# A fused attention and convolution block: the depthwise convolution and the line scans spread over VectorE, ScalarE and GpSimd

## The chip, the cores and the metric

The kernel runs on one core of one Trainium2 chip. The metric is the device time of one execution in microseconds, lower is better; three executions were timed. The engines are called PE (TensorE), DVE (VectorE), ACT (ScalarE), POOL (GpSimd) and SP (SyncE, which here issues all DMAs).

## The reference

Two layers work on `x` of shape (2, 56, 56, 384), all in float32. Layer 0 is neighborhood attention (12 heads, 7 x 7 window) and an MLP with GELU; it is not touched by the change except for one detail of its norm. Layer 1 is what matters:

```
def _L1_conv_ref(x, n1_g, n1_b, w_in, b_in, k_conv, on_g, on_b, w_out, b_out, n2_g, n2_b, w1, b1, w2, b2):
    h = _layernorm(x, n1_g, n1_b)
    p = h @ w_in + b_in                      # 384 -> 768 channels
    local = conv_general_dilated(p, k_conv, padding='SAME', feature_group_count=768)   # 3 x 3, depthwise
    lr = _ema_scan(local, axis=2)            # y[t] = 0.6 y[t-1] + 0.4 x[t], along the row
    rl = _ema_scan(local, axis=2, reverse=True)
    tb = _ema_scan(local, axis=1)            # down the column
    bt = _ema_scan(local, axis=1, reverse=True)
    mixed = 0.25 * (lr + rl + tb + bt) + local
    mixed = _layernorm(mixed, on_g, on_b)
    x = x + (mixed @ w_out + b_out)
    h2 = _layernorm(x, n2_g, n2_b)
    return x + gelu(h2 @ w1 + b1) @ w2 + b2
```

## The kernel before

The program has an attention part (about the first 1010 us of the span) and then two passes over the 6272 tokens in 13 groups of 512 (the last has 128).

*First half (layer 0's MLP and layer 1's projection in).* For each group: `hidden` makes 12 tiles of 128 hidden channels (PE, line L569, evicted with GELU by ACT at L578), `tokens` multiplies them back (L585, four tiles of 128 tokens, DVE adds the residual into `xc` at L720), the result is normed (`Norm`, `finish`) and, one group later, `project_in` makes six tiles of 128 channels of `p` (L569 again, evicted by ACT at L691) and stores them to `p_d` in DRAM. `Norm.add` takes statistics on DVE (L144, L145), `close` computes the reciprocal root (L149 on DVE, `pow` on POOL at L150), `apply` norms on DVE (L154).

*Second half.* `load_mix` brings the mixed image back, `measure` transposes it (L753) and takes statistics, `project_out` multiplies by `w_out` (L585, L765), then come norm, `hidden`, `tokens` and the output (L804). `add_row` adds a bias row on POOL (L518).

*The convolution* of one image is `phase_c(b)`: a Python generator that runs over six tiles of 128 channels. Each tile holds the whole 56 x 56 image per channel. Per tile: the image is loaded (`pt`); the centre tap is a product on DVE (L629, two halves of 28 rows); eight more taps are multiply-adds on DVE into `loc` (L640, each in two halves); ACT copies `loc` turned, in four pieces, into the buffer of `pt`, now called `lt` (L651); DVE scans 14 lines at a time forwards (L606), scales the line ends (L609), scans backwards in place (L611) and adds the share of it to `loc` (`mix`, L617: along rows from `both`, along columns with a stride from `lt`); the result goes to `mix_d` (L666). `loc` and `pt` share three buffers under the tag `image`.

*The order.* `Beside` mixes the generator's steps into the program behind the matmul work: `beside.go(worth)` credits 0.9 of the matmul time, and each `yield` debits the time of a step. `begin(phase_c(0))` stands in `project_in` where image 0 of `p` is complete (L701), `begin(phase_c(1))` at L783, behind `project_out(0)`; `end()` (L775, L799) flushes what is left before its result is loaded. The scheduling pass behind the language then orders each engine's queue by its own estimate, so the trace shows the norm's statistics between taps. Engines run their queues in order.

Of the kernel before, what the change touches and what calls it, by code (L numbers as in the profile page):

```python
# [104 lines left out]
def block_kernel(ctx: ExitStack, tc: tile.TileContext, ins: dict, out: bass.AP):  # L105
# [18 lines left out]
    nc.sync.dma_start(out=chan, in_=ins["chan"])  # L124
    mhalf = const.tile([P, NT], F32, name="mhalf")
    nc.vector.memset(mhalf, -0.5)

    def col(name, i=0):
        return chan[:, COL[name] + i : COL[name] + i + 1]

    class Norm:
# [14 lines left out]

        def close(self, k, n=P):
            rs = self.rs[:n, :k]
            nc.vector.tensor_scalar_add(rs, self.mv[:n, :k, 1], EPS)  # L149
            nc.gpsimd.tensor_tensor(rs, rs, mhalf[:n, :k], ALU.pow)  # L150

        def apply(self, k, x, out):
            n = x.shape[0]
            nc.vector.tensor_scalar(  # L154
                out, x, self.mv[:n, k, 0:1], self.rs[:n, k : k + 1], ALU.subtract, ALU.mult
            )

    def to_channels(psum, xs, dst, nch, g, b):
# [346 lines left out]
    nc.sync.dma_start(out=w_in, in_=ins["L1_conv_w_in"].rearrange("(c p) n -> p c n", p=P))  # L505
    load_w2(w2, s2)
    xs[1] = load_group(x1f, 1, "xa")
    rows = wp.tile([P, 3, C], F32, name="rows")
    for r in range(3):
        nc.sync.dma_start(out=rows[:, r, :], in_=ins["rows"][r + 2 : r + 3, :].to_broadcast([P, C]))  # L510
    w_out = wp.tile([P, NI, C], F32, name="w_out")
    nc.sync.dma_start(out=w_out, in_=ins["L1_conv_w_out"].rearrange("(c p) n -> p c n", p=P))

    def row(name):
        return rows[:, ROWS[name] - 2, :]

    def add_row(x, n, name):
        nc.gpsimd.tensor_tensor(  # L518
# [15 lines left out]
    def prepare_w_out():  # L534


        wide = wp.tile([P, P], F32, name="wide")
        ps = ps_y.tile([P, C], F32, name="y")
        for c in range(NI):
            nc.vector.tensor_copy(wide, col("L1_conv_on_b", c).to_broadcast([P, P]))  # L540
            nc.tensor.matmul(ps, lhsT=wide, rhs=w_out[:, c, :], start=c == 0, stop=c == NI - 1)
        nc.vector.tensor_tensor(row("b_out"), ps, row("b_out"), ALU.add)
        ps = ps_y.tile([P, C], F32, name="y")
        mean = wp.tile([P, P], F32, name="mean")
        nc.vector.memset(mean, 1.0 / INNER)
        for c in range(NI):
            nc.vector.tensor_scalar_mul(w_out[:, c, :], w_out[:, c, :], col("L1_conv_on_g", c))
            nc.tensor.matmul(ps, lhsT=mean, rhs=w_out[:, c, :], start=c == 0, stop=c == NI - 1)
        for c in range(NI):
            nc.vector.tensor_tensor(w_out[:, c, :], w_out[:, c, :], ps, ALU.subtract)  # L550

    def finish(norm, x, n):

        norm.close(n)
        xn = io.tile([P, NT, C], F32, name="xn")
        for k in range(n):
            norm.apply(k, x[:, k, :], xn[:, k, :])
        return xn

    def channels(xn, n, g, b):  # L560
# [13 lines left out]

    def hidden(w1, m, hT, n, b1):
        ps = columns(w1, m, hT, n)
        t = gp.tile([P, MT], F32, name="hid")
        nc.scalar.activation(t[:, : n * P], ps[:, : n * P], AF.Gelu, bias=col(b1, m))  # L578
        return t

# [9 lines left out]

    def phase_c(b):

        def load(m):
            t = cp.tile([P, H, W], F32, name="pt", tag="image")
            nc.sync.dma_start(out=t.rearrange("p h w -> p (h w)"), in_=p_d[b][m])
            return t

        tail = 1.0 / (1.0 - DECAY * DECAY)
        share = 0.25 * GAIN / tail / (1.0 + 0.5 * GAIN)

        def both_ways(dst, line):
            flat = dst.rearrange("p a b -> p (a b)")
            nc.vector.tensor_tensor_scan(  # L606
                flat, decay, line.rearrange("p a b -> p (a b)"), 0.0, ALU.mult, ALU.add
            )
            nc.vector.tensor_scalar_mul(dst[:, :, W - 1 :], dst[:, :, W - 1 :], tail)  # L609
            yield 2.1  # L610
            nc.vector.tensor_tensor_scan(  # L611
                flat[:, ::-1], decay, flat[:, ::-1], 0.0, ALU.mult, ALU.add
            )
            yield 1.8

        def mix(dst, s):
            nc.vector.scalar_tensor_tensor(dst, s, share, dst, ALU.mult, ALU.add)  # L617

        ready = load(0)
        for m in range(NI):  # L620
            pt = ready
            loc = cp.tile([P, H, W], F32, name="loc", tag="image")

            def tap(dy, dx):
                i = ((dy + 1) * 3 + dx + 1) * NI + m
                return taps[:, i : i + 1]

            for r in range(0, H, H // 2):
                nc.vector.tensor_scalar_mul(  # L629
                    loc[:, r : r + H // 2], pt[:, r : r + H // 2], tap(0, 0)  # L630
                )
                yield 1.0
                for dy in (-1, 0, 1):
                    for dx in (-1, 0, 1):
                        if dy == 0 and dx == 0:
                            continue
                        lo, hi = max(r, -dy), min(r + H // 2, H - max(0, dy))
                        xs, xt = max(0, -dx), max(0, dx)
                        n = W - abs(dx)
                        nc.vector.scalar_tensor_tensor(  # L640
                            loc[:, lo:hi, xs : xs + n], pt[:, lo + dy : hi + dy, xt : xt + n],
                            tap(dy, dx), loc[:, lo:hi, xs : xs + n], ALU.mult, ALU.add,
                        )
                        yield 1.8
            if m + 1 < NI:
                ready = load(m + 1)

            lt = pt.rearrange("p h w -> p (h w)").rearrange("p (w h) -> p w h", h=H)
            cuts = [slice(i, i + LINES) for i in range(0, W, LINES)]
            for i in cuts:  # L650
                nc.scalar.copy(lt[:, i, :], loc[:, :, i].rearrange("p h w -> p w h"))  # L651
            done = None
            for i in cuts:
                both = cp.tile([P, LINES, W], F32, name="both", bufs=2)
                yield from both_ways(both, loc[:, i, :])
                if done is not None:
                    mix(*done)
                    yield 1.0
                done = loc[:, i, :], both
            mix(*done)  # L660
            yield 1.0
            for i in cuts:
                yield from both_ways(lt[:, i, :], lt[:, i, :])
                mix(loc[:, :, i].rearrange("p h w -> p w h"), lt[:, i, :])
                yield 1.6
            nc.sync.dma_start(out=mix_d[b][m], in_=loc.rearrange("p h w -> p (h w)"))  # L666


# [16 lines left out]
    def project_in(g, xn):  # L685
        t0, n = groups[g]
        hT = channels(xn, n, "L1_conv_n1_g", "L1_conv_n1_b")
        pt = io.tile([P, NI, MT], F32, name="mx")
        for m in range(NI):
            ps = columns(w_in, m, hT, n)  # L690
            nc.scalar.activation(  # L691
                pt[:, m, : n * P], ps[:, : n * P], AF.Identity, bias=col("L1_conv_b_in", m)
            )
            beside.go(PRO)
        for b, at, here, n in images(t0, n * P):
            nc.sync.dma_start(
                out=p_d[b][:, :, at : at + n].rearrange("m p t -> p m t"),
                in_=pt[:, :, here : here + n],
            )
            if at + n == T1 and b == 0:  # L700
                beside.begin(phase_c(0))  # L701
# [73 lines left out]
    beside.end()  # L775
    ahead = load_mix(0)
    project_in(*waiting)
    load_w2(w2, s2)
    for k in range(groups[0][1]):
        measure(ahead[0], ahead[2], k)  # L780
    ahead[2].close(groups[0][1])
    x3, xn = project_out(0, *ahead)
    beside.begin(phase_c(1))  # L783
    ahead = load_mix(1)
    for k in range(groups[1][1]):
        measure(ahead[0], ahead[2], k)
# [2 lines left out]
    for g, (t0, n) in enumerate(groups):  # L789
        hid = []  # L790
        for m in range(NHID):
            hid.append(hidden(w1, m, hT, n, "L1_conv_b1"))
            beside.go(MLP)
        res = x3
        if g < last:
            x3, xn = project_out(g + 1, *ahead)
        if g + 2 <= last:
            if groups[g + 2][0] + groups[g + 2][1] * P > T1:
                beside.end()  # L799
            ahead = load_mix(g + 2)  # L800
        for k in range(n):
            ps = tokens(hid, w2, k)
            o = io.tile([P, C], F32, name="o")
            nc.vector.tensor_tensor(o, ps, res[:, k, :], ALU.add)  # L804
            nc.sync.dma_start(out=yout[t0 + k * P : t0 + (k + 1) * P, :], in_=o)
            if g + 2 <= last and k < groups[g + 2][1]:
                measure(ahead[0], ahead[2], k)
            beside.go(ROW)
        if g + 2 <= last:
            ahead[2].close(groups[g + 2][1])  # L810
        if g < last:
            hT = channels(xn, groups[g + 1][1], "L1_conv_n2_g", "L1_conv_n2_b")
# [62 lines left out]
```

## Time and profile before

| | |
|---|---|
| median of 3 runs | 3246.63 us (3242.19 to 3247.16) |
| profiled execution, its own time | 3243.59 us |
| its span, first to last instruction | 3241.5 us |
| PE busy | 2961.1 us, 91% |
| DVE busy | 1673.4 us, 52% |
| ACT busy | 934.0 us, 29% |
| POOL busy | 405.2 us, 13% |
| convolution taps on DVE, L640 | 338.3 us, 192 instructions |
| waits of ACT's turned copies (L651) for the taps | 219.3 us, 9 times |

Busy time is the union of an engine's instructions; a busy engine may be waiting inside an instruction. "Idle before" names what the engine waited for. In a row such as `loc<-pt,taps,loc` the output tile stands first. `128x784` is 128 partitions by 784 elements, that is 14 lines of 56. Durations of one DVE instruction overlap the next by some 0.08 us in the records.

### The profile page before, as it was taken

How to read it: one execution, taken by the hardware profiler on the slowest of the kernel's cores; microseconds unless marked ns; L12 is line 12 of the kernel's file. 1: busy time of each engine (PE TensorE's matmuls, PEld its weight loads, DVE VectorE, ACT ScalarE, POOL GpSimd, SP SyncE). 2: the span in 40 equal slices, each digit the busy share in tenths (PEclk: the TensorE clock that was granted, in tenths of full speed). 3: DMA queues.
4: the chain of work that ended last, by engine and by line, in shares of the span. 5: the costliest groups of instructions: out<-in, count | busy, mean ns of one | idle time of the engine just before them, and what ended most of it. 6: DMA issues, size and time to landing. Idle time of an engine off the chain costs nothing. (4 is left out here: it accounts for less than half of the span.)

```text
span 3241.5 us, 35452 instructions
## 1 busy us (share of the span) xinstructions
PE 2961.1 (91%) x13647; PEld 1621.3 (50%) x13647; DVE 1673.4 (52%) x3371; ACT 934.0 (29%) x2269; POOL 405.2 (13%) x277
## 2 busy tenths in 40 slices
PE   6999999999987999999998668688787799999999
PEld 3555555555554555555554334444444455555555
DVE  3555555555562111111199999689999951111110
ACT  1555555455562222222222122221022111111111
POOL 2310123300031000000001000011110111111000
PEclk9999999999998999999999889798988899999999
DMA  6222222211123111111212211332221121111000
GB/s 136 74 59 64 64 64 77 62 54 58 60 63 120 39 39 39 39 39 39 79 40 79 98 59 52 108 134 79 76 74 47 42 76 39 39 39 39 17 10 13
DMA packets 105673, 197.03 MB, mean 61 GB/s; under 512 B 7408, under 2 KB 81120, under 8 KB 102432
## 3 DMA queue, kind: packets, MB, share of 16 engines
q1 hardware_dynamic: 105504, 194.77, 18.4%
q8 instruction: 107, 1.75, 0.2%
q14 instruction: 62, 0.51, 0.0%
HBM read 117.68 MB, written 77.07 MB: 60 GB/s over the span
## 5 line engine op out<-in xcount | busy, mean ns | idle before, releaser
L585 PE MATMUL y<-w,hid 128*128 128x384 f32 x2352 | 786.9, 494 | 58.2 <-DVE xc L720 58.2
L569 PE MATMUL mm<-hT,w 128*128 128x512 f32 (+1 forms) x1872 | 770.4, 572 | 7.5 <-ACT hid L578 4.6
L585 PEld LDWEIGHTS y<-w,hid 128*128 128x128 f32 x2352 | 450.1, 194 | 365.4 <-DVE xc L720 61.8
L569 PEld LDWEIGHTS mm<-hT,w 128*128 128x128 f32 x1872 | 346.1, 192 | 418.4 <-issue 395.9
L578 ACT ACTIVATE hid<-mm,chan 128x512 f32<-128x512 f32 (+1 forms) x312 | 206.1, 663 | 850.2 <-PE mm L569 850.2
L346 ACT ACTIVATE pr<-pr,nm 112x238 f32<-112x238 f32 (+3 forms) x672 | 326.8, 488 | 227.2 <-DVE nm L339 224.2
L150 POOL TENSOR_TENSOR rs<-rs,mhalf 128x4 f32<-128x4 f32 (+2 forms) x66 | 85.9, 1302 | 2023.6 <-DVE rs L149 1978.6
L640 DVE SCALAR_TENSOR_TENSOR loc<-pt,taps,loc 128x1485 f32<-128x1485 f32 (+2 forms) x192 | 338.3, 1803 | 0.0
L339 DVE CUSTOM_DVE_ANT_0 pr<-sc,bias 112x238 f32<-112x238 f32 (+3 forms) x672 | 240.6, 407 | 171.6 <-PE sc L330 167.2
L167 ACT ACTIVATE hT<-tp,chan 128x512 f32<-128x512 f32 (+2 forms) x159 | 110.0, 744 | 669.5 <-PE tp L164 645.5
L720 DVE TENSOR_TENSOR xc<-y,xa 128x384 f32<-128x384 f32 x49 | 27.0, 551 | 500.5 <-PE y L585 500.5
L585 PE MATMUL y<-w_out,mx 128*128 128x384 f32 x588 | 208.4, 510 | 40.1 <-DVE xc L765 40.1
L360 PE MATMUL pt<-ident,pr 112*100 112x112 f32 (+5 forms) x1584 | 210.4, 272 | 10.2 <-ACT pts L365 10.2
L232 PE MATMUL tp<-hT,wqkv 128*128 128x448 f32 x504 | 211.9, 553 | 8.1 <-DVE qT L238 5.4
L569 PE MATMUL mm<-hT,w_in 128*128 128x512 f32 (+1 forms) x468 | 194.3, 574 | 18.1 <-ACT mx L691 18.1
L360 PEld LDWEIGHTS pt<-ident,pr 112*100 112x100 f32 (+5 forms) x1584 | 163.7, 148 | 82.1 <-issue 53.4
L765 DVE SCALAR_TENSOR_TENSOR xc<-y,rs,xa 128x384 f32<-128x384 f32 x49 | 29.8, 609 | 303.9 <-PE y L585 302.8
L585 PEld LDWEIGHTS y<-w_out,mx 128*128 128x128 f32 x588 | 115.7, 200 | 124.6 <-DVE xc L765 44.4
L164 PE MATMUL tp<-ident,xn 128*128 128x128 f32 (+1 forms) x609 | 88.1, 290 | 83.9 <-DVE xn L154 51.5
L330 PE MATMUL sc<-kT,qT 32*112 32x238 f32 (+3 forms) x1344 | 158.1, 418 | 0.0
L569 PEld LDWEIGHTS mm<-hT,w_in 128*128 128x128 f32 x468 | 87.2, 192 | 120.7 <-issue 93.1
L404 PE MATMUL tp<-wproj,oT 128*112 128x384 f32 x336 | 129.8, 525 | 15.7 <-DVE qT L238 14.7
(70 smaller groups left out, 2710.1 us busy)
## 6 DMA issues: line engine op xcount, KB each, us to landing
pt<-p_d SPq DMA_DIRECT2D x12, 1568.0 KB
mix_d<-loc SPq DMA_DIRECT2D x12, 1568.0 KB
xa<-x_d SPq DMA_DIRECT2D x24, 768.0 KB
p_d<-mx SPq DMA_DIRECT2D x11, 1536.0 KB
mx<-mix_d SPq DMA_DIRECT2D x11, 1536.0 KB
xg<-in_x SPq DMA_DIRECT2D x14, 672.0 KB
v_d<-vs SPq DMA_DIRECT2D x56, 168.0 KB
xr<-in_x SPq DMA_DIRECT2D x56, 168.0 KB
```

Of the source, the lines that this page charges most:

```text
L164: nc.tensor.transpose(tp[:, k * n : (k + 1) * n], x[:, c * P : (c + 1) * P], ident[:n, :n])
L167: nc.scalar.activation(dst[:, c, : len(xs) * n], tp, AF.Identity, bias=col(b, c), scale=col(g, c))
L232: nc.tensor.matmul(ps, lhsT=wqkv[:, c, m * P : (m + 1) * P], rhs=hT[:, c, :], start=c == 0, stop=c == NC - 1,)
L330: nc.tensor.matmul(ps[:, : w.nk], lhsT=qTs[w.b, w.g][d, hg, w.j, :], rhs=kT[d, hg, w.r0 : w.r0 + w.kr, w.c0 : w.c0 + w.kc], start=True, st ...
L339: nc.vector.tensor_tensor_reduce(out=self.pr[:, i, : w.nk], in0=ps[:, : w.nk], in1=w.bias[:, 4 * hg + i, : w.nk], scale=-1.0, scalar=BIG, ...
L346: nc.scalar.activation(self.pr[:, i, : w.nk], self.pr[:, i, : w.nk], AF.Exp, bias=nm[:, i : i + 1], scale=-1.0, accum_out=w.sums[:, h : h ...
L360: nc.tensor.transpose(tp[:n, i, :], self.pr[:, i, a : a + n], idt)
L404: nc.tensor.matmul(ps, lhsT=w.oT[:, c, :], rhs=wproj[:, c, :], start=c == 0, stop=c == NC - 1)
L569: nc.tensor.matmul(ps[:, : n * P], lhsT=w[:, c, m * P : (m + 1) * P], rhs=hT[:, c, : n * P], start=c == 0, stop=c == NC - 1,)
L578: nc.scalar.activation(t[:, : n * P], ps[:, : n * P], AF.Gelu, bias=col(b1, m))
L585: nc.tensor.matmul(ps, lhsT=t[:, k * P : (k + 1) * P], rhs=w[:, m, :], start=m == 0, stop=m == len(lhs) - 1,)
L640: nc.vector.scalar_tensor_tensor(loc[:, lo:hi, xs : xs + n], pt[:, lo + dy : hi + dy, xt : xt + n], tap(dy, dx), loc[:, lo:hi, xs : xs + n ...
```

## The change

In `phase_c` the centre tap is now four ACT copies scaled by the tap, in pieces of 14 rows. Five taps stay on DVE. The other three are made in pieces of 14 rows: ACT writes the product into a small tile (tag `piece`, four buffers), POOL adds it to `loc`. While DVE has the upper half of the image POOL has the lower, then they change over. ACT writes scaled copies of the rows (`line`, also tag `piece`) and scaled turned copies (`turn`); DVE scans them in place; POOL adds the scans to `loc` (`add`, `add_column`) where DVE's `mix` did. The credits of the `yield`s change with it.

In `finish` the norm is applied by ACT as scale and bias, with the bias made by two POOL products (`shifts`), and `close` adds epsilon on POOL. This holds for the three norms that pass through `finish`. The generator for image 1 begins ahead of `project_out(0)`. The rest makes room in the on-chip memory: two bias rows instead of three, with `b2_1` loaded later over `b2_0`; `wide` and `mean` in the buffers of the hidden tiles; the output added in place.

```
         def close(self, k, n=P):
             rs = self.rs[:n, :k]
-            nc.vector.tensor_scalar_add(rs, self.mv[:n, :k, 1], EPS)
+            nc.gpsimd.tensor_tensor(rs, self.mv[:n, :k, 1], eps[:n, :k], ALU.add)
             nc.gpsimd.tensor_tensor(rs, rs, mhalf[:n, :k], ALU.pow)
...
+        def shifts(self, k):
+            self.sh = self.small.tile([P, NT], F32, name="sh")
+            nc.gpsimd.tensor_tensor(self.sh[:, :k], self.mv[:, :k, 0], minus[:, :k], ALU.mult)
+            nc.gpsimd.tensor_tensor(self.sh[:, :k], self.sh[:, :k], self.rs[:, :k], ALU.mult)
+
+        def apply_by_scalar(self, k, x, out):
+            nc.scalar.activation(
+                out, x, AF.Identity, bias=self.sh[:, k : k + 1], scale=self.rs[:, k : k + 1]
             )
...
         norm.close(n)
+        norm.shifts(n)
         xn = io.tile([P, NT, C], F32, name="xn")
         for k in range(n):
-            norm.apply(k, x[:, k, :], xn[:, k, :])
+            norm.apply_by_scalar(k, x[:, k, :], xn[:, k, :])
...
-        def mix(dst, s):
-            nc.vector.scalar_tensor_tensor(dst, s, share, dst, ALU.mult, ALU.add)
+        def forth(t):
+            flat = t.rearrange("p a b -> p (a b)")
+            nc.vector.tensor_tensor_scan(flat, decay, flat, 0.0, ALU.mult, ALU.add)
+            end = t[:, :, W - 1 :]
+            nc.vector.scalar_tensor_tensor(end, end, tail - 1.0, end, ALU.mult, ALU.add)
+
+        def back(t):
+            flat = t.rearrange("p a b -> p (a b)")[:, ::-1]
+            nc.vector.tensor_tensor_scan(flat, decay, flat, 0.0, ALU.mult, ALU.add)
+
+        def add(dst, t):
+            nc.gpsimd.tensor_tensor(dst, dst, t, ALU.add)
+
+        cuts = [slice(i, i + LINES) for i in range(0, H, LINES)]
+        by_vector = [(-1, 0), (1, 0), (0, -1), (0, 1), (-1, -1)]
+        by_gpsimd = [(-1, 1), (1, -1), (1, 1)]
...
+            def gpsimd_taps(pieces):
+                for piece in pieces:
+                    for at in by_gpsimd:
+                        (r, c), (rt, ct) = reach(piece, *at)
+                        t = cp.tile([P, LINES, W], F32, name="tmp", tag="piece", bufs=4)
+                        t = t[:, : r.stop - r.start, : c.stop - c.start]
+                        nc.scalar.activation(t, pt[:, rt, ct], AF.Copy, scale=tap(*at))
+                        add(loc[:, r, c], t)
+                        yield
+
+            for half in (0, 1):
+                if half == 0:
+                    for i in (2, 0, 1, 3):
+                        nc.scalar.activation(
+                            loc[:, cuts[i]], pt[:, cuts[i]], AF.Copy, scale=tap(0, 0)
                         )
+                others = gpsimd_taps(cuts[2:] if half == 0 else cuts[:2])
+                for at in by_vector:
+                    next(others, None)
+                    (r, c), (rt, ct) = reach(slice(half * H // 2, (half + 1) * H // 2), *at)
+                    nc.vector.scalar_tensor_tensor(
+                        loc[:, r, c], pt[:, rt, ct], tap(*at), loc[:, r, c], ALU.mult, ALU.add
+                    )
+                    yield 2.1
+                for _ in others:
+                    yield 1.0
...
+            def line(i):
+                rows[i] = cp.tile([P, LINES, W], F32, name="row", tag="piece", bufs=4)
+                nc.scalar.activation(rows[i], loc[:, cuts[i]], AF.Copy, scale=share)
+
+            def turn(i):
+                nc.scalar.activation(
+                    lt[:, cuts[i], :], loc[:, :, cuts[i]].rearrange("p h w -> p w h"), AF.Copy,
+                    scale=share,
+                )
+
+            def add_column(i):
+                add(loc[:, :, cuts[i]], lt[:, cuts[i], :].rearrange("p w h -> p h w"))
+
+            for i in (2, 3, 0, 1):
+                line(i)
+            for i in range(4):
+                turn(i)
+            for k, i in enumerate((2, 3, 0, 1)):
+                forth(rows[i])
+                yield 2.1
+                back(rows[i])
+                yield 1.8
+                if k > 0:
+                    add(loc[:, cuts[j]], rows[j])
+                j = i
+            for k in range(4):
+                forth(lt[:, cuts[k], :])
+                yield 2.1
+                if k == 0:
+                    add(loc[:, cuts[j]], rows[j])
+                back(lt[:, cuts[k], :])
+                yield 1.8
+                if k > 0:
+                    add_column(k - 1)
+            yield 2.0
+            add_column(3)
+            yield 2.0
...
     project_in(*waiting)
+    load_row(0, "b2_1")
+    beside.begin(phase_c(1))
     load_w2(w2, s2)
...
     x3, xn = project_out(0, *ahead)
-    beside.begin(phase_c(1))
...
-            o = io.tile([P, C], F32, name="o")
-            nc.vector.tensor_tensor(o, ps, res[:, k, :], ALU.add)
+            o = res[:, k, :]
+            nc.vector.tensor_tensor(o, ps, o, ALU.add)
```

More of the change, by code (lines that the diff above doesn't have):

```diff
@@ L126, in block_kernel @@
     nc.vector.memset(mhalf, -0.5)
+    minus = const.tile([P, NT], F32, name="minus")
+    nc.vector.memset(minus, -1.0)
+    eps = const.tile([P, NT], F32, name="eps")
+    nc.vector.memset(eps, EPS)
     def col(name, i=0):
@@ L507, in block_kernel, with load_row @@
     xs[1] = load_group(x1f, 1, "xa")
-    rows = wp.tile([P, 3, C], F32, name="rows")
-    for r in range(3):
-        nc.sync.dma_start(out=rows[:, r, :], in_=ins["rows"][r + 2 : r + 3, :].to_broadcast([P, C]))
+    rows = wp.tile([P, 2, C], F32, name="rows")
+    def load_row(i, name):
+        r = ROWS[name]
+        nc.sync.dma_start(out=rows[:, i, :], in_=ins["rows"][r : r + 1, :].to_broadcast([P, C]))
+    load_row(0, "b2_0")
+    load_row(1, "b_out")
     w_out = wp.tile([P, NI, C], F32, name="w_out")
@@ L514, in row @@
     def row(name):
-        return rows[:, ROWS[name] - 2, :]
+        return rows[:, 1 if name == "b_out" else 0, :]
     def add_row(x, n, name):
@@ L534, in prepare_w_out @@
     def prepare_w_out():
-        wide = wp.tile([P, P], F32, name="wide")
+        wide = gp.tile([P, MT], F32, name="wide", tag="hid")[:, :P]
         ps = ps_y.tile([P, C], F32, name="y")
@@ L543, in prepare_w_out @@
         ps = ps_y.tile([P, C], F32, name="y")
-        mean = wp.tile([P, P], F32, name="mean")
+        mean = gp.tile([P, MT], F32, name="mean", tag="hid")[:, :P]
         nc.vector.memset(mean, 1.0 / INNER)
@@ L576, in hidden @@
         ps = columns(w1, m, hT, n)
-        t = gp.tile([P, MT], F32, name="hid")
+        t = gp.tile([P, MT], F32, name="hid", tag="hid")
         nc.scalar.activation(t[:, : n * P], ps[:, : n * P], AF.Gelu, bias=col(b1, m))
@@ L602, in phase_c, with reach @@
         share = 0.25 * GAIN / tail / (1.0 + 0.5 * GAIN)
[L604 to L614, printed above, removed]
-        def mix(dst, s):
-            nc.vector.scalar_tensor_tensor(dst, s, share, dst, ALU.mult, ALU.add)
+        def forth(t):
[11 more added lines that the diff above has]
+        by_gpsimd = [(-1, 1), (1, -1), (1, 1)]
+        def reach(rows, dy, dx):
+            lo, hi = max(rows.start, -dy), min(rows.stop, H - max(0, dy))
+            xs, xt, n = max(0, -dx), max(0, dx), W - abs(dx)
+            return (slice(lo, hi), slice(xs, xs + n)), (slice(lo + dy, hi + dy), slice(xt, xt + n))
         ready = load(0)
@@ L626, in tap @@
                 return taps[:, i : i + 1]
[L628 to L642, printed above, removed]
-                        )
-                        yield 1.8
+            def gpsimd_taps(pieces):
[12 more added lines that the diff above has]
+                            loc[:, cuts[i]], pt[:, cuts[i]], AF.Copy, scale=tap(0, 0)
+                        )
+                others = gpsimd_taps(cuts[2:] if half == 0 else cuts[:2])
[8 more added lines that the diff above has]
+                    yield 1.0
             if m + 1 < NI:
@@ L648, in phase_c @@
             lt = pt.rearrange("p h w -> p (h w)").rearrange("p (w h) -> p w h", h=H)
[L649 to L665, printed above, removed]
+            rows = {}
+            def line(i):
[5 more added lines that the diff above has]
+                    scale=share,
+                )
+            def add_column(i):
[24 more added lines that the diff above has]
+            yield 2.0
             nc.sync.dma_start(out=mix_d[b][m], in_=loc.rearrange("p h w -> p (h w)"))
```

## The prediction

> **What bounds the kernel now.** The profiled execution took 3243.59 us (span 3241.5, so 2.1 us lie around it); the median of the runs is 3246.63. I make all sums against 3243.6; the median is 3 us above. I read first the span in 40 slices, then busy time by stage.
>
> ```profile
> PE   6999999999987999999998668688787799999999
> DVE  3555555555562111111199999689999951111110
> ```
>
> PE is full except at two places, slices 21 to 26 and 27 to 33, and exactly there DVE is full. These are the two convolution phases (`phase_c(0)` and `phase_c(1)`), worked off beside the matmuls. I cut the stages at the first and last convolution instruction. The columns are the stage, its length, then busy us (instructions) of PE, weight loads, DVE, ACT, POOL, then granted clock, DMA share and GB/s.
>
> ```profile
> 1010.00:1610.00 600.00, 599.88 (x1708) 308.61 (x1707) 89.54 (x241) 124.28 (x182) 46.03 (x24) 1.00 0.11 39
> 1610.00:2072.00 462.00, 368.51 (x1061) 192.98 (x1059) 448.35 (x423) 105.86 (x132) 30.81 (x12) 0.90 0.19 68
> 2138.00:2626.00 488.00, 392.90 (x1117) 209.64 (x1116) 479.59 (x453) 89.31 (x99) 59.29 (x19) 0.90 0.16 60
> 2626.00:3241.00 615.00, 611.69 (x1928) 340.34 (x1926) 98.90 (x235) 78.69 (x120) 57.35 (x29) 1.00 0.10 35
> ```
>
> DVE works 448 of 462 and 480 of 488 us there. PE could be quicker: a group of 512 tokens takes 79.9 us in the quiet part of the first half (the same `pow` at 1319.47 and 1399.40 us in the timeline) and 81.3 in the second (chain of waits, 2670.24 to 2751.52). The first phase holds some 28 + 4 x 80 = 348 us of PE time, so 114 are lost; in the second, five groups take from 2142.04 to 2670.24, 528 for 406, so 122 are lost. That 236 us is all that relieving DVE can bring.
>
> **The view that decides.** The change moves work from DVE to POOL. So I looked at what the two do to each other, in the few places where POOL adds in a convolution phase. Two stretches of the timeline, DVE and POOL apart (start, us, engine, line):
>
> ```profile
> 1877.51 1.81 DVE L640 SCALAR_TENSOR_TENSOR loc<-pt,taps,loc 128x1540 f32<-128x1540 f32 x1
> 1879.24 3.41 DVE L609 TENSOR_SCALAR both<-both 128x14 f32<-128x14 f32 x1
> 1882.57 1.78 DVE L606 TENSOR_TENSOR_SCAN both<-decay,loc 128x784 f32<-128x784 f32 x1
> ...
> 1877.73 4.89 POOL L518 TENSOR_TENSOR xa<-xa,rows 128x1536 f32<-128x1536 f32 x1 [1.81 <-issue]
> ...
> 2209.24 1.02 DVE L144 BATCH_NORM_STATS2 st<-xi 128x6 f32<-128x384 f32 x2
> 2210.17 3.58 DVE L611 TENSOR_TENSOR_SCAN pt<-decay,pt 128x784 f32<-128x784 f32 x1
> 2213.67 0.18 DVE L145 BATCH_NORM_AGGREGATE mv<-st 128x2 f32<-128x12 f32 x1
> 2213.77 4.86 DVE L611 TENSOR_TENSOR_SCAN pt<-decay,pt 128x784 f32<-128x784 f32 x1
> ...
> 2207.09 5.01 POOL L518 TENSOR_TENSOR xc<-xc,rows 128x1536 f32<-128x1536 f32 x1 [1.76 <-DVE pt L609]
> 2212.07 4.91 POOL L518 TENSOR_TENSOR xa<-xa,rows 128x1536 f32<-128x1536 f32 x1
> ```
>
> The POOL add takes 3.43 us in the quiet part. Issued while a tap runs on DVE it takes 4.89: the tap's remaining 1.5 and its own 3.4. A 14-element DVE operation behind it then takes 3.41 instead of 0.14, to the instant the add ends. The scan at 2213.77 takes 4.86 for its usual 1.78. They exclude each other whole and take turns. The statistics at 2209.24, one input each, run at their usual 0.5 us inside the first add (L609 has one tensor input too and waited, so this isn't so for every one-input form). So in the phases the resource is not DVE but the **path shared by DVE's taps and scans and by POOL's adds**, and I sum the turns on it.
>
> ```profile
> L518 POOL TENSOR_TENSOR xa<-xa,rows 128x1536 f32<-128x1536 f32 x9 | 30.8, 3427 | 28.2 <-issue 15.5 <-DVE st L144 10.9 <-DVE xn L154 1.8
> L518 POOL TENSOR_TENSOR xc<-xc,rows 128x384 f32<-128x384 f32 x1 | 1.0, 992 | 0.6 <-DVE xn L154 0.6
> L617 DVE SCALAR_TENSOR_TENSOR loc<-both,loc 128x784 f32<-128x784 f32 x48 | 48.1, 1020 | 1.9 <-ACT pt L651 1.9
> L617 DVE SCALAR_TENSOR_TENSOR loc<-pt,loc 128x784 f32<-128x784 f32 x48 | 76.9, 1610 | 0.3
> ```
>
> (groups by shape, the first from 1010 to 1610 us: busy us, mean ns.) These two adds give the price line: 0.99 us at 384, (3.43 - 0.99) / 1152 = 2.12 ns for each element more, so 1.84 us at 784, 1.81 at 770, 1.69 at 715.
>
> [...]
>
> **The change, per phase of six channel tiles.**
>
> Removed from DVE: the centre tap (12 times about 1.0), three of eight taps (36 x 1.72 = 62), the mixing (24 x 0.96 + 24 x 1.61 = 62), the norm applications L154 (12 to 13) and L149 (1.3): about 150 us. Kept on DVE with two inputs: 60 taps x 1.72 (15 in a row take 25.91 in the timeline) = 103; 96 scans x 1.70 from start to start = 163; 48 edge scalings x 0.08 = 4. Together 270. Scans read a pre-scaled copy instead of `loc`; same shape, no change.
>
> Added to POOL, per tile: 12 tap products added (nine of 770 elements, three of 715 at the image's edge) 21.4, four row adds and four column adds of 784, 14.7. That is 36.1, or 217 a phase. What DVE gave up there cost 62 + 62, so the same arithmetic holds the path longer than before.
>
> POOL's own work stays: L518 and L150, uncontended, 19 in the first phase and 43 in the second. Each `close` and `shifts` adds up to three tiny POOL operations, 24 and 19 in all. None is in the trace: between nothing and the 1.02 us of the `pow` on the same four columns; an add or product is less than a `pow`, I take 0.6: 14 and 11.
>
> Path held: 270 + 217 + 19 + 14 = 520 and 270 + 217 + 43 + 11 = 541. DVE's one-input work (L720, L144, L145: 34; with L765 and L804: 54) can run inside POOL's turns: between all and none hidden; I take half, 17 and 27.
>
> Bubbles: `loc` of the next tile lies in the buffer of the last `lt`, so ACT's centre pieces wait for the last column add, and DVE waits for three of them. ACT's price for 14 x 56 elements: L346 has 0.484 at 238 and 0.518 at 280, so 0.81 ns each over 0.29, 0.93 us. Three are 2.8 us, plus one scaled copy (0.93) ahead of the first scan. In program order behind those copies stand PE's evictions (`hid`, `mx`), and PE waits for them, but PE has 114 to spare. Nothing to 10 us a tile; I take 4, 24 a phase.
>
> So the phases last 520 + 17 + 24 = 561 and 541 + 27 + 24 = 592, against 462 and 488: **+99 and +104**.
>
> Around them: `phase_c(1)` begins ahead of `project_out(0)` instead of behind. The store of `p_d` goes out at 2114.2, its load needs some 8 us, the first tap stands now at 2140.95: nothing to 15 earlier, I take 12. The load of `b2_1` and the earlier image load pass `load_w2` on SP's queue, whose weights are first used a hidden layer (31 us) later: nothing, unless that lead is gone. The norm by ACT: add, `pow`, two products on POOL, then four ACT applications of some 0.45 us, in ACT's queue ahead of the next `hid` evictions. Three PSUM buffers of 2.57 us give PE 7.7 us of cover; statistics 1.4, POOL 3.5, ACT 1.9 and the eviction 0.7 make 7.5, and the next tile's norm follows. In the first half nothing to 3 us a group over 12 groups; I take 10 in all. In the second half the norm is needed one token stage (31 us) later, so nothing. The writing in place of the output and the shared `hid` buffers cost nothing: nothing waits for them within a group.
>
> 3243.6 + 99 + 104 - 12 + 10 = 3444.6, say **3445 us**. All low ends: 58 + 53 - 15 gives 3340. High ends: one-input work unhidden, 10 us bubbles, 1.02 for each tiny operation, and column adds dearer by 0.65 us for their stride (as L617's two shapes differ), +178 and +191, with 36 for the norms: 3649.
>
> **Rivals.**
> (A) *POOL's adds run beside DVE.* For it: DVE alone then has 270 + 34, under PE's 348, and PE sets the end. 236 come back; each tile's burst on ACT, four copies of 0.93 and four turns of 1.66, 10.4 us against the cover of 7.7 to 5.1, costs some 5 us where it falls in the 58% of a group that needs ACT: 12 x 5 x 0.58 = 35, and 10 for the norms: 3053 us. Against it: every overlap shown. The change stops being slower where an add holds the path under (462 - 344) / 120 = 0.98 us; the row says 1.84.
> (B) *A ring of waits on top.* ACT waits for a free `piece` buffer (four, released by POOL), evictions stand behind it, PE behind them, DVE's `xc` behind PE, so that the path lies idle. Today ACT's `pt` copies already wait 219 us for L640 with evictions behind them. At 20 us a tile instead of 4, 192 more: 3637. Against it: DVE's taps need nothing from PE, and the products run a tile ahead.
> (C) *No difference to be measured*, within 0.2% (6.5 us, about what a measurement can tell): the port sum and the 236 would have to cancel by chance.
>
> **Chances.** Forecast 0.80, A 0.09, B 0.09, C 0.02. The range of 8 in 10 goes from 3310, a little under the low ends, to 3600, which leaves out most of B and all of A. Slower 0.89, same 0.02, faster 0.09.
>
> **What would show it.** In the changed profile: stretches of some 560 and 590 us with DVE records stretched (taps from 1.75 to above 2.5 us each, scans likewise), POOL adds recorded well above 1.84 us, the PE slices there lower than now; the rest of the span as before, 600 and 615 us stretches within 10. Wrong if POOL's adds stay at 1.84 and taps at 1.75 while they overlap (A), or if DVE and POOL both idle for long in the phases with ACT waiting (B).

## The result and the profile after

The changed kernel takes 3537.07 us (median of 4 runs, 3532.68 to 3542.2) against 3244.93 us for the kernel before: a ratio of 1.0901, 95% interval 1.0882 to 1.092. It is some 292 us slower. The span of the profiled execution is 3540.3 us, 298.8 longer than before.

The page of the changed kernel, the span in 40 slices:

```profile
PE   6999999999879999997655559854656699999999
DVE  3555555555611110006897870378889611111110
POOL 2300123100310001005777770367777411111000
```

Counted from 1, the two convolution phases are slices 19 to 24 and 26 to 32. PE falls to 7, 6 and then 5 tenths in the first and to between 4 and 6 in the second (slice 26 is half still the stretch between), where it kept 6 to 9 before. DVE is no longer full; POOL's row is at 7 in the middle of both. In numbers (busy time by stage: length, then PE, weight loads, DVE, ACT, POOL, granted clock, DMA share, GB/s; first phase, the stretch between, second phase, the rest of the span):

```profile
1612.00:2132.00 520.00, 310.85 (x746) 151.74 (x745) 424.99 (x272) 201.34 (x240) 385.50 (x147) 0.79 0.15 56
2132.00:2254.00 122.00, 121.03 (x392) 66.28 (x391) 9.12 (x22) 30.86 (x54) 8.76 (x16) 1.00 0.23 81
2254.00:2800.00 546.00, 315.12 (x892) 170.36 (x890) 449.60 (x320) 184.86 (x216) 390.99 (x155) 0.80 0.17 64
2800.00:3540.00 740.00, 733.59 (x2283) 405.19 (x2283) 102.20 (x228) 119.61 (x182) 75.90 (x72) 0.99 0.09 33
```

Two things are to be seen in the first phase and around it. DVE does fewer instructions and is busy almost as long: 272 for 425 us, where it did 423 in 448. And between the phases stand 122 us of full PE with an idle convolution, where the kernel before had 66; behind the second phase stand 740, where it had 615. That is PE work that the phases did not cover. The granted clock in the phases fell from 0.90 to 0.79 and 0.80; PE has idle time there, and what the clock alone costs was not tested. What became of the instructions (groups by shape: busy us, mean ns, idle before), first in the kernel before:

```profile
L640 DVE SCALAR_TENSOR_TENSOR loc<-pt,taps,loc 128x1540 f32<-128x1540 f32 x96 | 172.7, 1828 | 0.0
L611 DVE TENSOR_TENSOR_SCAN pt<-decay,pt 128x784 f32<-128x784 f32 x48 | 93.3, 1945 | 0.1
L609 DVE TENSOR_SCALAR pt<-pt 128x14 f32<-128x14 f32 x48 | 10.7, 227 | 0.0
```

Then in the changed kernel:

```profile
L679 DVE SCALAR_TENSOR_TENSOR loc<-pt,taps,loc 128x1540 f32<-128x1540 f32 x60 | 162.3, 2706 | 0.5
L635 DVE TENSOR_TENSOR_SCAN pt<-decay,pt 128x784 f32<-128x784 f32 x48 | 159.7, 3328 | 0.3
L631 DVE SCALAR_TENSOR_TENSOR pt<-pt 128x14 f32<-128x14 f32 x48 | 33.8, 705 | 0.0
L638 POOL TENSOR_TENSOR loc<-loc,tmp 128x770 f32<-128x770 f32 x108 | 309.2, 2884 | 67.8 <-ACT tmp L665 55.3 <-ACT loc L672 10.6
```

A tap of the same shape took 1.83 us before and takes 2.71; the backward scan of the columns 1.95 before and 3.33; a scaling of 14 elements 0.23 before and 0.71 (it is another instruction now, with two tensor inputs); an add priced at 1.81 is recorded with 2.88. Both engines' records hold the time that they wait for the other. One turn after the other, in the timeline of DVE and POOL (start, us):

```profile
1685.25 3.37 DVE L635 TENSOR_TENSOR_SCAN pt<-decay,pt 128x784 f32<-128x784 f32 x1
1688.54 3.35 DVE L631 SCALAR_TENSOR_TENSOR pt<-pt 128x14 f32<-128x14 f32 x1
1691.82 1.78 DVE L629 TENSOR_TENSOR_SCAN pt<-decay,pt 128x784 f32<-128x784 f32 x1
...
1680.22 6.75 POOL L638 TENSOR_TENSOR loc<-loc,row 128x784 f32<-128x784 f32 x2
1686.92 4.93 POOL L538 TENSOR_TENSOR xa<-xa,rows 128x1536 f32<-128x1536 f32 x1
```

The 14-element scaling begins at 1688.54 and ends at 1691.9, when the bias add ends. The add itself was issued at 1686.92 and had to wait for the scan that ended at 1688.6; from there it took 3.2 us.

The effect reaches PE through two engines. From the waits (engine and line, what for: us in total, times, longest), the first line of the kernel before, the others of the changed one:

```profile
PEld mm L569 <- ACT hid L578: 7.4, 4, 3.1
...
ACT tmp L665 <- POOL loc L638: 260.8, 109, 10.6
PEld mm L590 <- ACT hid L599: 161.2, 30, 15.2
```

ACT's products wait for a buffer that POOL's adds release, the evictions stand behind them, and PE waits for the evictions, which it hardly did before (at 1646.35 us PE stops for 3.14 us, until the eviction of 1648.77, which ACT runs after two products that waited 5.89 and 2.36 us for POOL's adds); and PE's weight loads wait 86.2 us for the residual add on DVE, where they waited 61.8 before. So two explanations are open: the **holding** of the path shared by DVE and POOL (H, the forecast's), and the **chain of waits** between ACT, POOL and DVE as such (W, its rival). The 122 us between the phases suggest a third, the **order** (O): how much matmul work the compiled program puts beside each phase.

### The profile page after: what moved, and what is told of

The parts are those of the page before. It is cut to its first block, busy times and chain, and to the rows that moved or that the text cites. A ratio compares the mean times of both kernels' runs of the same rounds, so it can differ in the third digit from the quotient of the medians.

```text
span 3540.3 us, 35895 instructions
## 1 busy us (share of the span) xinstructions
PE 3009.4 (85%) x13647; PEld 1635.3 (46%) x13647; DVE 1572.0 (44%) x2968; ACT 1223.5 (35%) x2656; POOL 1118.2 (32%) x661
## 4 chain that ended last, share of the span: by engine, by line
PE 25%; DVE 12%; POOL 9%; issue 3%; ACT 1%; DMA 0%; POOLq 0%; DVEq 0%; ACTq 0%
PE y L606 13%; PE mm L590 10%; POOL loc L638 7%; DVE pt L635 3%; DVE loc L679 2%; DVE row L629 2%; DVE row L635 2%; DVE pt L629 2%; DVE row L631 1%; PE xi L815 1%; PE tp L179 0%; ACT loc L672 0%; POOL rs L154 0%; POOL xa L538 0%; DVE st L148 0%
## 5 line engine op out<-in xcount | busy, mean ns | idle before, releaser
L590 PE MATMUL mm<-hT,w 128*128 128x512 f32 (+1 forms) x1872 | 813.8, 595 | 145.2 <-ACT hid L599 136.2
L606 PEld LDWEIGHTS y<-w,hid 128*128 128x128 f32 x2352 | 452.3, 195 | 402.9 <-DVE xc L782 86.2
L590 PEld LDWEIGHTS mm<-hT,w 128*128 128x128 f32 x1872 | 358.2, 200 | 586.3 <-issue 402.0
L153 POOL TENSOR_TENSOR rs<-mv,eps 128x4 f32<-128x4 f32 (+2 forms) x66 | 25.3, 383 | 1312.8 <-DVE mv L149 1312.8
L638 POOL TENSOR_TENSOR loc<-loc,tmp 128x770 f32<-128x770 f32 (+1 forms) x144 | 391.5, 2737 | 126.5 <-DVE loc L679 56.9
L679 DVE SCALAR_TENSOR_TENSOR loc<-pt,taps,loc 128x1540 f32<-128x1540 f32 (+3 forms) x120 | 297.1, 2494 | 120.2 <-ACT loc L672 60.8
L326 POOL TENSOR_TENSOR xr<-xr,rows_a 112x384 f32<-112x384 f32 x56 | 56.5, 1010 | 624.3 <-DMA xr<-in_x 457.7
L169 ACT ACTIVATE xn<-xc,sh,rs 128x384 f32<-128x384 f32 x98 | 61.4, 696 | 479.0 <-POOL sh L166 479.0
L665 ACT ACTIVATE tmp<-pt,taps 128x770 f32<-128x770 f32 (+1 forms) x144 | 131.5, 923 | 260.9 <-POOL loc L638 260.8
L638 POOL TENSOR_TENSOR loc<-loc,row 128x784 f32<-128x784 f32 x48 | 147.6, 3092 | 98.6 <-ACT pt L696 58.7
```

The lines of the kernel that those rows point to most:

```text
L590: nc.tensor.matmul(ps[:, : n * P], lhsT=w[:, c, m * P : (m + 1) * P], rhs=hT[:, c, : n * P], start=c == 0, stop=c == NC - 1,)
L606: nc.tensor.matmul(ps, lhsT=t[:, k * P : (k + 1) * P], rhs=w[:, m, :], start=m == 0, stop=m == len(lhs) - 1,)
L638: nc.gpsimd.tensor_tensor(dst, dst, t, ALU.add)
L665: nc.scalar.activation(t, pt[:, rt, ct], AF.Copy, scale=tap(*at))
L679: nc.vector.scalar_tensor_tensor(loc[:, r, c], pt[:, rt, ct], tap(*at), loc[:, r, c], ALU.mult, ALU.add)
```

## Experiments

All but e8 and e12 are one execution each, beside 3240.42 us (first four), 3243.69 (second four) or 3243.76 (last four) for the kernel before. That kernel's own executions lie between 3236.7 and 3248.7, so a difference of some 10 us between single times says nothing.

**e1, the adds shrunk, the waits kept.** Part of the computation is left out: each add of the convolution takes the first element of each line only.

```
-            nc.gpsimd.tensor_tensor(dst, dst, t, ALU.add)
+            nc.gpsimd.tensor_tensor(dst[:, :, :1], dst[:, :, :1], t[:, :, :1], ALU.add)
```

> Every POOL add of the convolution is cut to the first element of each of its 14 lines, so most of the adding is left out; every wait between ACT, POOL and DVE stays. Theory H (the holding of the path shared by DVE's two-input instructions and POOL's adds costs the time): an add then holds it some 0.3 us instead of 1.8, the path sum falls from 520 to about 345 a phase, taps are recorded near 1.75 us again, and the time is 3170 to 3250 us. Theory W (the chain of waits costs the time, ACT product to POOL add to buffer, with PE's evictions behind): waits are as before and it stays above 3400.

Measured 3192.93 us: 344 less than the changed kernel, inside H's range. From the groups:

```profile
L679 DVE SCALAR_TENSOR_TENSOR loc<-pt,taps,loc 128x1540 f32<-128x1540 f32 x60 | 109.4, 1823 | 0.6
L638 POOL TENSOR_TENSOR loc<-loc,tmp 128x14 f32<-128x14 f32 x108 | 63.9, 617 | 96.1 <-ACT tmp L665 64.4 <-ACT loc L672 31.6
```

Taps are back at 1.82 us. Each add still waits for its product, each buffer still for its add; the dependences exist and cost little as long as an add is short. But a short add shortens the waits too: ACT waits 76 us for POOL instead of 261. So e1 shows that the length of the adds decides, and not yet whether it does so through the path or through the waits. The next run parts the two.

**e2, the scans taken off the path.** The scans' constant lies in PSUM, so each has one input in SBUF.

```
+    ps_d = ctx.enter_context(tc.tile_pool(name="psd", bufs=1, space=PSUM))
...
-    decay = wp.tile([P, LINES, W], F32, name="decay")
+    decay = ps_d.tile([P, LINES // 2, W], F32, name="decay")
...
+            for h in (slice(0, LINES // 2), slice(LINES // 2, LINES)):
+                flat = t[:, h, :].rearrange("p a b -> p (a b)")
                 nc.vector.tensor_tensor_scan(flat, decay, flat, 0.0, ALU.mult, ALU.add)
...
```

> The constant operand of the scans (decay) lies in PSUM, so a scan has one input in SBUF; scans are cut to 7 lines for it to fit one bank, and the transposes have two PSUM buffers instead of three. Theory H: scans no longer exclude POOL's adds, scan time of 163 us a phase runs beside the row and column adds, 400 to 430 us of path a phase, 3250 to 3350 us; a scan that overlaps an add keeps its own length (some 0.9 us for 392 elements). Theory W: the waits are unchanged, 3500 us or more.

Measured 3380.72 us, 156 less than the changed kernel: far under W's 3500, and 31 above the range that I gave H. Adds and dependences are those of the changed kernel, and ACT still waits 230 us for POOL. The mechanism shows in the timeline:

```profile
1686.84 1.84 DVE L638 TENSOR_TENSOR_SCAN pt<-decay,pt 128x392 f32<-128x392 f32 x2
1688.59 1.81 DVE L631 TENSOR_TENSOR_SCAN pt<-decay,pt 128x392 f32<-128x392 f32 x2
1690.44 0.65 DVE L633 SCALAR_TENSOR_TENSOR pt<-pt 128x14 f32<-128x14 f32 x1
...
1688.76 2.29 POOL L641 TENSOR_TENSOR loc<-loc,pt 128x784 f32<-128x784 f32 x1 [1.99 <-DVE pt L638]
```

Of the two scans at 1688.59 the second runs wholly inside a POOL add, 0.9 us long like the first. The two-input scaling at 1690.44 ends when the add ends. The add, 2.29 us here, is a column add: the 48 of this run take 2.28 in the mean, and the row adds 1.84. With e1 this shows H; W alone has fallen. The price missed by 31 us in what stayed: two scans of 7 lines take some 1.80 us from start to start against 1.70 for one of 14 lines, which makes 10 us a phase; the scalings still wait; and the order was as tight as in the changed kernel (next). How the 31 us divide among these was not measured.

**e3, the order alone.** No arithmetic is changed. Each step of the convolution is queued behind the latest eviction on ACT and the latest residual add on DVE that stand ahead of it in the program.

```
+    def step(self):
+        with ExitStack() as held:
+            for ins in self.marks.values():
+                held.enter_context(self.tc.issue_after(ins))
+            return next(self.work, None)
...
-            step = next(self.work, None)
+            step = self.step()
...
+        beside.mark("act", nc.scalar.activation(t[:, : n * P], ps[:, : n * P], AF.Gelu, bias=col(b1, m)))
...
```

> Each step of the convolution is queued on ACT behind the latest eviction and on DVE behind the latest residual add that stand ahead of it in the program, so that the compiled order spreads six tiles over 4.3 groups of matmul work instead of 3.3; no arithmetic is changed. Theory O (part of the loss is that the compiled order puts the six tiles beside too little PE work, 263 us in the first phase): the path sum of 520 stands beside some 340 us of PE work, loss 180 to 200 a phase, 3390 us (3340 to 3450). Theory W, or no part for the order: 3500 us or more.

Measured 3343.77 us: 193 less than the changed kernel, with the same instructions of the same sizes. O holds, and weighs more than I gave it. The groups of the first half are counted from 0 here. In the kernel before, the first residual add of group 7 and the last of group 11 stand at:

```profile
1614.27 0.56 DVE L720 TENSOR_TENSOR xc<-y,xa 128x384 f32<-128x384 f32 x1 [44.38 <-PE y L585]
2067.59 0.54 DVE L720 TENSOR_TENSOR xc<-y,xa 128x384 f32<-128x384 f32 x1
```

In the changed kernel the first residual adds of groups 7 to 10 come 165, 172 and 169 us after one another:

```profile
1615.50 0.56 DVE L782 TENSOR_TENSOR xc<-y,xa 128x384 f32<-128x384 f32 x1 [47.92 <-PE y L606]
1780.02 0.53 DVE L782 TENSOR_TENSOR xc<-y,xa 128x384 f32<-128x384 f32 x1
1951.64 0.53 DVE L782 TENSOR_TENSOR xc<-y,xa 128x384 f32<-128x384 f32 x1
2120.57 0.53 DVE L782 TENSOR_TENSOR xc<-y,xa 128x384 f32<-128x384 f32 x1
```

The last scan of the phase stands ahead of the last of them. Three groups, 240 us of PE at its quiet pace, passed in 505. In e3 the first residual adds of groups 7 to 11 come at 1613.5, 1723.2, 1834.7, 1946.3 and 2059.3, four groups in 446 us; the first and the last:

```profile
1613.49 0.56 DVE L793 TENSOR_TENSOR xc<-y,xa 128x384 f32<-128x384 f32 x1 [47.96 <-PE y L617]
2059.34 0.56 DVE L793 TENSOR_TENSOR xc<-y,xa 128x384 f32<-128x384 f32 x1 [9.62 <-PE y L617]
```

The convolution phases themselves are no shorter in e3: 545 and 556 us from the first centre copy to the last column add, against 505 and 532 in the changed kernel. But 1108 and 1259 matmuls run inside them, against 703 and 807; in the kernel before it was 1049 and 1102.

**e4, e5, e6, which part costs.** e4 has all eight taps and all eight line adds on DVE (both edits below), e5 the taps alone (the first edit), e6 the line adds alone (the second); the credits of a tile are kept in sum.

```
-        by_vector = [(-1, 0), (1, 0), (0, -1), (0, 1), (-1, -1)]
-        by_gpsimd = [(-1, 1), (1, -1), (1, 1)]
+        by_vector = [(-1, 0), (1, 0), (0, -1), (0, 1), (-1, -1), (-1, 1), (1, -1), (1, 1)]
+        by_gpsimd = []
...
-            nc.gpsimd.tensor_tensor(dst, dst, t, ALU.add)
+            nc.vector.tensor_tensor(dst, dst, t, ALU.add)
```

> All eight taps as DVE multiply-adds and all eight line adds on DVE; POOL has none of the convolution; ACT keeps the centre tap, the scaled copies and the norms; the credits of a tile are the same in sum. Theory H: path per tile 16 taps 27.5, scans 27.2, adds some 10, together 65 us, 393 a phase and 33 of POOL's own, beside some 300 us of PE work: 3260 to 3330 us, near the kernel before. Theory W alone: nothing waits for POOL any more and ACT still does 14.6 us of work a tile less: under 3200.

> All eight taps on DVE; POOL keeps the eight line adds a tile; credits of a tile the same in sum. Theory H with O (path sum less the PE work that the compiled order puts beside it): 332 of taps and scans, 99 of line adds (column adds measured at 2.28 us each, row adds 1.84), 33 of POOL's own, beside some 300 us: loss 164 a phase, 3336 us (3280 to 3390). Theory W: half of the chain of waits is gone, halfway to the all-DVE kernel and no relation to the path sum.

> The eight line adds on DVE, three taps stay as ACT products added by POOL. Theory H with O: 270 + 60 on DVE, 128 of tap adds, 33 of POOL's own, 491 beside some 265 us: loss 226 a phase, 3460 us (3400 to 3500): the taps are the dearer half of the move. If taps and line adds cost alike: as e5.

Measured 3245.02, 3345.40 and 3409.48 us. e5 is where the path sum put it; e4 is 15 us under the lower end of its range, nearer to it than to W's (under 3200); e6 is in its range. So from e4 the line adds on POOL cost 100 us, the three taps on POOL 164, and both together 292, 27 more than their sum. e4 is level with the kernel before (3240.42 beside it), so the rest of the change nets nothing: the loss comes with the adds that POOL took over.

**e7, the norms alone**, in the kernel before (the `close`, `shifts` and `apply_by_scalar` of the change).

> The kernel before with the norm part of the change alone: epsilon added by POOL, shift by two POOL products, three norms applied by ACT. My forecast's terms: 0 to 36 us of stalls in the first half (10 taken), less some 25 us of DVE work taken out of the two convolution phases: 3215 to 3265. Rival: the applications block ACT's queue ahead of the evictions in every group: above 3280.

Measured 3214.94 us, 29 less than before and at the lower end of the range: this part is a gain. In the changed kernel the first residual add of group 7 comes at 1615.50 against 1614.27 before, and the groups ahead of it are 79.9 us apart in both kernels: the longer chain of the norm costs nothing in a group of the quiet part.

**e8, taps on DVE, e2's scans, e3's order**, in four executions.

> All taps on DVE, the scans' constant in PSUM (so that POOL's line adds run beside the scans), the compiled order spread by the queueing of e3. Theories H and O together: DVE 55 us a tile, 332 + 34 a phase, POOL 132 beside it, against some 340 us of PE work: 3060 to 3150 us, faster than both kernels. Were either theory wrong by much: no better than the all-DVE kernel's 3245.

Measured 3189.17 us (3181.84 to 3191.19), ratio 0.9823, 0.9806 to 0.9839: 1.8% faster than the kernel before, but 39 us over the range. DVE's sum was priced too low: 192 taps came to 366 us and 384 half scans to 352 by the groups of its profile, 183 and 176 a phase where I had 165 and 163, and the scalings still waited for POOL's adds.

**e9 and e10, the order again**: e3's queueing in e4 and in e7.

> e4 (no POOL work in the convolution) with the queueing of e3. Theory O: the compiled order now puts 340 us of PE work beside each phase instead of 300, 40 us less a phase: 3165 (3140 to 3200). If order only matters where POOL is loaded: 3245 as e4.

> e7 (the kernel before with the norms by ACT) with the queueing of e3. The compiled order of the kernel before already puts 343 us of PE work beside the first phase; the queueing moves the sixth tile by one token stage at most. Theory O: little, 3180 to 3220. If the queueing itself (rather than the spread) brought e3's gain: under 3150.

Measured 3201.55 (43 less than e4, just over the range) and 3267.82 us (53 more than e7: a miss, on the side that I had not thought of). The page of e10:

```profile
PE   6999999999987999999989997189999619999999
DVE  3555555555561100010288889979999881111110
```

PE is at 1 tenth in one slice of each phase's end: the queueing spreads this kernel's tiles too thin, groups run at 84 to 90 us, and what is left of the convolution is then flushed with PE idle (from 2000 to 2150 us PE is busy 49 us and DVE 127). More spread is not better; the work beside a phase has to match the phase.

**e11 and e12, the scalings too.** e11 is e8 with the factor of the line ends in PSUM; e12 is e11 with the credits times 1.15.

```
...
-            nc.vector.scalar_tensor_tensor(end, end, tail - 1.0, end, ALU.mult, ALU.add)
+            nc.vector.tensor_tensor(end, end, tails, ALU.mult)
...
```

> e8 with the factor of the line ends in PSUM, so that the 14-element scalings have one input in SBUF too. Theory H: the scalings fall from some 0.55 us to 0.25 or less in the mean, 4 us a tile less on DVE, which is what bounds e8's phases: 3130 to 3165. If they still wait for POOL's adds: 3185.

> e11 with the credits of a step times 1.15, so that the tiles spread evenly over each phase's groups. Theory O: at or below e11, 3110 to 3160, the fastest of all.

The groups of e8 and of e11:

```profile
L644 DVE SCALAR_TENSOR_TENSOR pt<-pt 128x14 f32<-128x14 f32 x48 | 28.1, 586 | 1.4
```

```profile
L646 DVE TENSOR_TENSOR pt<-pt,decay 128x14 f32<-128x14 f32 x48 | 8.6, 180 | 1.3
```

The scaling falls from 0.59 to 0.18 us. e11 takes 3164.35 us (one execution, 79 under the kernel before's median beside it), the fastest of all and at the upper end of its range. e12 takes 3219.28 (3218.52 to 3220.4; ratio 0.9931, 0.9915 to 0.9948), 55 more than e11 and a miss: the even spread leaves a flush like e10's (from 2040 to 2125 us PE is busy 27).

## Why the prediction was right, and where its sum was off

*Right: direction and mechanism.* That POOL's adds and DVE's taps and scans take turns on one path was read from a handful of overlaps. e1 shows that the length of the adds decides (344 us), e2 that an operand moved out of SBUF ends the exclusion for the scans alone (156 us, with the dependences kept). So what those overlaps showed held for whole phases in the changed kernel, and in e2 the scans of 7 lines, with one input in SBUF, did not contend: the 192 backward ones take 0.92 to 0.98 us each, two of them 1.84 beside the row adds (from 1672.79) and 1.84 with POOL idle (from 1691.12). Rival A, adds beside DVE for nothing, is out: in the changed kernel taps are recorded with 2.71 us and adds with 2.88, and e1's taps are back at 1.82.

*Roughly right, with terms off: the length of a phase.* The forecast held the path for 520 and 541 us, and with 17 and 27 us for DVE's one-input work and 24 for bubbles came to 561 and 592. In the trace the first phase runs from the first centre copy at 1618.0 to the end of the last column add at 2123.0, 505 us; the second takes 532 (2272.2 to 2804.3). So the forecast's phases are 56 and 60 us too long (16 and 36 by e3's, which hold more matmul work). Some of its terms can be read: the tiny POOL operations take 0.2 us uncontended, not 0.6 (0.20 and 0.21 in e2's timeline); a column add alone takes 2.28, not 1.84 (e2); a row add 1.84 as priced. And a turn on the path is shorter than the same instruction alone. Where the two engines alternate in the changed kernel, a tap takes 1.62 us in the median from the end of the add ahead of it (alone 1.72 from start to start), a tap's add 1.68 from the end of the tap (alone 1.82), the bias add shown above 3.2 (alone 3.43). Over 120 adds and 156 taps and scans a phase that makes some 30 us, an estimate from these differences. How the rest divides between one-input work and bubbles was not measured.

*Failed: "against 462 and 488: +99 and +104".* The lengthening of a phase is the loss only if the same matmul work stands beside it, and the text took the 348 us of the kernel before for granted. The changed program put three groups beside the first phase instead of more than four, and PE had to do the rest afterwards, alone. From group 7's first residual add to group 10's last it is 523.5 us for 263 at quiet pace: 260 us lost, against 110 before (1614.27 to 2067.59 for 343). That is +150 in the first phase where I had +99. To the first `xc` of `project_out(0)` (2268.42 against 2123.11) the changed kernel is 145 us behind, from there to the end another 153, where I had 104 - 12. One of the forecast's own signs failed with it: the rest of the span was to stay within 10 us, and the stretch behind the second phase is 740 us for 615. e3 shows what the order is worth: with no other change it gives back 193 us. Why the scheduling pass packed the tiles so is argued, not shown: its estimate knows DVE's shorter list, and not the turns on the path.

*Partly luck: the number.* The two errors have opposite signs. In e3, with at least as much matmul work beside the phases as in the kernel before, they last 545 and 556 us, 52 in all less than the forecast's. A straight line between the changed kernel (1510 matmuls beside its two phases, 297 us lost against 3240.42) and e3 (2367 matmuls, 103 lost) gives some 150 us of loss at the 2151 matmuls of the kernel before. This is an estimate; the sum had 201. So the price that the sum did carry was some 50 us too high, and the order, which was no term of it, cost some 145 more. The total came as near as it did because the one made up for part of the other.

*Mis-sized: the norms.* I took 10 us for stalls in the first half; the quiet groups show none, and e7 has the part as a gain of 29, of which my sum had about 25 in the DVE work removed. The application on ACT was priced at 0.45 us, though the text's own price line for ACT gives 0.60 at 384 elements; it takes 0.70 in the changed kernel, and no cost of it is to be seen in the quiet groups.

*Held: the earlier start.* From the last store of `p_d` to the first convolution instruction of the second phase it is 26.7 us before (2114.2 to 2140.95) and 10.7 after (2261.5 to 2272.2), 16 us less where I took 12. What it brings by itself was not tried.

*Rival B, the ring of waits.* Its waits are in the trace (ACT 261 us for POOL), but e2 keeps the dependences and most of these waits (230 us), and 156 us are gone. The waits pass the path's delay on to PE; they are not its cause.

Sum of it: from 3243.7, the norms bring it to 3215 (e7); the rest of the change (ACT's centre tap and copies, the earlier start, the order that comes of them) to 3245 (e4); taps and line adds on POOL to 3537. e4's 30 us over e7 are less than the 43 that the order alone gives back in e9, but no run separates the order from the centre tap there.

## What to carry to other kernels

Before moving elementwise work from DVE to POOL, look in the trace for the places where the two overlap already, and count operands: here the taps, with two inputs in SBUF, took turns with POOL's adds (1.83 us before, 2.71 in the changed kernel), and a row add of 784 elements took 1.84 us on POOL against some 0.96 on DVE, so moving it lengthened the sum. With their constant operand in PSUM the scans left that path (156 us in e2), the scalings, with their factor there too, fell from 0.59 us (e8) to 0.18 (e11), and then POOL's help was worth having: e11, with the line adds on POOL, takes 37 us less than e9, with everything on DVE (single executions). When beside-work shrinks or grows, check how many groups of matmul the compiled order puts beside it: in this kernel order alone was worth 193 us one way (e3) and 53 the other (e10).

## What the runs showed that was not expected

- A POOL add that reads one input at a stride of 56 elements took 2.28 us against 1.84 for the same 784 elements in order (e2, where no scan contends).
- POOL adds and products on 4 columns took 0.2 us (e2), five times less than the `pow` of 1.02 on the same columns.
- Where DVE and POOL alternated in the changed kernel, a turn was 0.1 to 0.2 us shorter than the instruction alone (a tap's add 1.68 for 1.82).
- A 14-element DVE instruction took 3.35 us in the changed kernel (at 1688.54), to the end of POOL's bias add. With its second operand in PSUM it took 0.18 in the mean (e11).
